# A four-layer graph attention network: moving the residual's end to GpSimd and shifting the preparation of some steps

## The chip, the cores and the metric

The kernel runs on one core of a Trainium2 chip. The metric is the device time of one execution in microseconds (us), as the median of several runs; less is better. The core has a matrix engine (TensorE, PE in the profile), a vector engine (VectorE, DVE), an activation engine (ScalarE, ACT), a general engine (GpSimd, POOL), a queue engine that issues transfers (SyncE, SP), and DMA engines. Each executes its own list of instructions in order, and they wait for each other by semaphores.

## The reference

Sixteen graphs (batches) of N = 1024 nodes with F = 256 features share one adjacency matrix. Four layers follow each other; each is

```
h   = max(layernorm(x), 0)
q   = h @ W                                    # heads: 4 of width 64 (layers 0, 2) or 1 of 256 (layers 1, 3)
e   = leaky_relu(e_src[i] + e_dst[j])          # e_src, e_dst = q times the two halves of a
att = softmax over j of e where adj[i, j], else -infinity
x   = x + elu(att @ q)                         # layers 0 to 2; relu instead of elu in layer 3
```

Layers 0 and 1 mask by adj > 0 and layers 2 and 3 by adj != 0. The slope of leaky_relu is 0.2, in layer 3 it is 0.01.

## The kernel before, in words

**Steps.** The work is cut into 64 steps, one for each pair of a graph and a layer. `order_of_steps` writes their order by hand: four streams, each of four graphs in turn, advance through the layers so that steps with four heads and steps with one head mostly alternate. The start is (graph, layer) = (0,0), (1,0), (2,0), (0,1), (3,0), (1,1), (2,1), (0,2), ..., and the end is step 57 (13,2), 58 (12,3), 59 (14,2), 60 (15,2), 61 (13,3), 62 (14,3), 63 (15,3). Only after steps 0, 1 and 59 does a step of four heads follow a step of four heads; the function `slack(n)` is true where one with one head follows.

**One step.** TensorE does the aggregation `att @ q` in eight groups (slots k = 0 to 7, L405). For each head and each of eight blocks of 128 source nodes, VectorE makes a tile w of 128 x 1024 weights (L389) from a broadcast row g, a column and the mask; 18 buffers ("w") hold such tiles. A step of four heads has 32 tiles, a step of one head 8, but both have about the same matrix work, so VectorE is the busier in the first kind and TensorE in the second, and the buffers carry the difference. ScalarE takes each group's sums from PSUM into y (L420). `finish(n)` then runs in the slots of the next step: a reciprocal of the softmax sums (L441, VectorE), the product y times r on GpSimd (L452; where `slack` and four heads, VectorE also makes min(y, 0) r at L451), the clamp min(y, 0) on GpSimd (L454), the exponential on ScalarE (L458), `max(e - 1, y)` on VectorE (L464) and the sum x + e on GpSimd (L465). The last layer has one VectorE instruction in place of the latter, `x = max(y, 0) + x` (L467), and then the store (L470) from SyncE, after which the next graph is loaded. Each of these comes twice, once for each half of the 1024 nodes.

**Preparation of a step** runs ahead, in 21 pieces: layernorm statistics of each half (L241, VectorE; four instructions a half), their combination on GpSimd (L268 to L280), normalising with relu (L286, ScalarE, four a half), a split into 16-bit halves (L295, ScalarE), a transposition by DMA (L297, issued by SyncE), a merge (L303, ScalarE), eight projections (L328, TensorE) with evictions on ScalarE (L330), exponentials for column and factor (L336, L338), a scaling on GpSimd (L340), the factors of the rows (L346, L347), a transposition of them (L352, L354) and a trip through DRAM (L356), from which they are fetched as rows gs (L372) and copied by ScalarE into PSUM as g (L384). In the steps n = 0 and 1 TensorE transposes instead (L317). Four PSUM banks ("bank") are shared by the group sums, the projections and the small transpositions, two more pairs hold g. Six buffers ("rows") are shared by normalised, split, turned and merged data and by e.

**What sets the order.** The program emits all instructions itself, in the order of emission for each engine. A table of 21 numbers says at which slot, counted from slot 8 (n - 2), each piece of step n's preparation is emitted: 0 and 1 are the statistics, 2 the combination, 3 and 4 normalising, 5 and 6 split and merge of half 0, 7 to 10 its projections, 11 to 16 the same for half 1, 17 to 20 the factors, rows and fetches. Steps with one head use ONE or TIGHT, with four heads SOON, FOUR, SHORT, NEXT; LATE is used where a step's input is finished too late (`free`). In each slot the order is: the w tiles that this group needs, the group, pieces of `finish`, broadcasts g, a weight piece from `later`, the preparation due, and more w tiles ahead. The start-up (masks, the first step's preparation) has a list of its own, `order`. `later` holds the pieces of `weight_columns` for layers 1 to 3: `vectors` fetches the attention vectors by a small DMA on SyncE (L143), `spread` broadcasts them by TensorE (L150, L153), `columns` and `bound` follow on VectorE, TensorE and GpSimd (L160, L161, L173 to L180).

Of the kernel before, what the change touches and what calls it, by code (L numbers as in the profile page):

```python
# [32 lines left out]
ALU = mybir.AluOpType  # L33
# [16 lines left out]
FOUR = (-8, -8, -5, 0, 1, 0, 3, 5, 5, 5, 5, 1, 4, 5, 5, 5, 5, 6, 8, 8, 10)  # L50
SHORT = (-4, -4, -4, 0, 1, 0, 3, 5, 5, 5, 5, 1, 4, 5, 5, 5, 5, 6, 8, 8, 10)
NEXT = (-4, -4, -4, 1, 3, 2, 5, 8, 8, 8, 8, 4, 7, 8, 8, 8, 8, 9, 10, 10, 12)
ONE = (2, 2, 2, 3, 4, 3, 5, 7, 7, 7, 7, 4, 7, 8, 8, 8, 8, 8, 11, 11, 12)
SOON = (0, 0, 0, 1, 2, 1, 3, 4, 4, 5, 5, 2, 5, 6, 6, 7, 7, 7, 8, 8, 10)
FIRST = (-4, -4, -4, -2, -0.9, -1, -1, -0.8, -0.8, -0.8, -0.8, 0, 0, 1, 1, 1, 1, 1, 2, 2, 4)
TIGHT = (4, 4, 4, 5, 6, 5, 7, 8, 8, 8, 8, 6, 8, 9, 9, 9, 9, 9, 10, 10, 12)
LATE = (0, 0, 0, 1, 2, 1, 3, 4, 4, 4, 4, 2, 4, 5, 5, 5, 5, 5, 6, 6, 8)


# [9 lines left out]
def kernel(ctx: ExitStack, tc: tile.TileContext, x, adj, ws, avs, out):  # L69
    nc = tc.nc  # L70
# [351 lines left out]
    def slack(n):  # L422

        return LAYERS[steps[n + 1][1]][0] == 1

    def finish(n):

        b, l = steps[n]
        H = LAYERS[l][0]
        D = F // H  # L430
        st = state[n]

        def views(half):
            s = slice(half * HALF, (half + 1) * HALF)
            return (xs[b][:, s, :].rearrange("p c (h d) -> p (c h) d", h=H),
                    st["y"][:, s, :, 0:D].rearrange("p c h d -> p (c h) d"),
                    st["r"][:, s, :].rearrange("p c h -> p (c h)"))

        def divide():
            st["r"] = small.tile([P, C, H], F32, name="r")  # L440
            nc.vector.reciprocal(st["r"], st["y"][:, :, :, D])  # L441

        def scaled(half):
            xh, yh, r = views(half)
            rb = r[:, :, None].to_broadcast([P, HALF * H, D])
            if l < L - 1:

                e = st["e", half] = prep.tile([P, HALF * H, D], F32, name="rows",
                                                    bufs=HBUFS)
                if H > 1 and slack(n):  # L450
                    nc.vector.scalar_tensor_tensor(e, yh, 0.0, rb, op0=ALU.min, op1=ALU.mult)  # L451
            nc.gpsimd.tensor_tensor(yh, yh, rb, op=ALU.mult)  # L452
            if l < L - 1 and not (H > 1 and slack(n)):
                nc.gpsimd.tensor_scalar(e, yh, 0.0, -3.0e38, op0=ALU.min, op1=ALU.max)  # L454

        def exponential(half):
            if l < L - 1:
                nc.scalar.activation(st["e", half], st["e", half], AF.Exp)  # L458

        def add(half):  # L460
            xh, yh, r = views(half)
            if l < L - 1:
                e = st["e", half]
                nc.vector.scalar_tensor_tensor(e, e, -1.0, yh, op0=ALU.add, op1=ALU.max)  # L464
                nc.gpsimd.tensor_add(xh, xh, e)  # L465
                return
            nc.vector.scalar_tensor_tensor(xh, yh, 0.0, xh, op0=ALU.max, op1=ALU.add)  # L467

        def store(half):
            nc.sync.dma_start(  # L470
                out=out[b].rearrange("(p c) f -> p c f", p=P)[:, half * HALF:(half + 1) * HALF],
                in_=xs[b][:, half * HALF:(half + 1) * HALF, :])
            if half == 1 and b + STREAMS < B:
                load(b + STREAMS)


        at = (0, 0, 0, 0, 1, 1, 1) if slack(n) and H > 1 else (0, 0, 1, 1, 2, 2, 3)
        return list(zip(at, (divide, lambda: scaled(0), lambda: scaled(1), lambda: exponential(0),
                             lambda: exponential(1), lambda: add(0), lambda: add(1)))) + (
                    [(4, lambda: store(0)), (4, lambda: store(1))] if l == L - 1 else [])  # L480

# [37 lines left out]
    def emit_heads(i):  # L519

        while done["g"] <= min(i + C // 2, done["tiles"] + C, len(tiles) - 1):
            n, h, _ = tiles[done["g"]]
            if n >= done["prepared"]:
                break
            broadcast(n, h)
            done["g"] += C
            fetch_heads()
# [13 lines left out]
    for n, (b, l) in enumerate(steps):  # L541

        free = -99
        if b % STREAMS in last:
            over = last[b % STREAMS] + 1
            free = 8 * over + (8 if l == 0 else 2 if LAYERS[steps[over][1]][0] == 1 else 4)
        last[b % STREAMS] = n
        start = 8 * (n - 2)
        kind = ONE if LAYERS[l][0] == 1 else SOON if n < 3 else FOUR
        if kind is FOUR and free > start + kind[0]:  # L550
            kind = SHORT if slack(n - 2) else NEXT
        if kind is ONE and free > start + kind[0]:
            kind = TIGHT
        if free > start + kind[0]:
            kind = LATE
            start = max(free, agenda_of[-1][0] + 5, start - LATE[7])
        agenda_of.append([start + k for k in kind] if n > 1 else FIRST)
        if n > 2:


            assert agenda_of[n][7] >= 8 * (n - 2)
            assert agenda_of[n][3] >= agenda_of[n - 1][12]
    ending = []
    later = {}
    with tc.manual_schedule():
        blocks = [mask_rows(c) for c in range(C)]
        layer = [weight_columns(l) for l in range(L)]
        layer[0][0](nc.scalar)
        load(0, 2)
        load_weights(0)  # L570
        for c in range(C):
            blocks[c][0]()
        load(1)
        load_weights(1)
        for i in range(2, STREAMS):
            load(i)
        nc.scalar.activation(warm, half1, AF.Exp)
        nc.vector.tensor_copy(identb, ident)
        layer[0][1]()
        first = [piece for _, piece in preparation(0)]  # L580

        order = (

            [first[0], first[1], first[3], lambda: layer[0][2](range(1)), first[2],
             lambda: layer[0][2](range(1, K)), first[5], first[6], first[4], layer[0][3]]

            + [blocks[c][1] for c in range(4)]
            + [first[7], first[8], blocks[0][2], blocks[4][1], blocks[5][1], blocks[0][3],
               first[9], first[10], blocks[1][2], blocks[6][1], blocks[7][1], blocks[1][3],
               first[11], first[12], blocks[2][2], blocks[0][4],  # L590
               lambda: prepare(-4), first[13], first[14], blocks[1][4], blocks[2][3],
               blocks[3][2], first[15], first[16], blocks[3][3]]

            + [first[17], blocks[4][2], first[18], first[19], lambda: emit_heads(0),
               blocks[5][2], blocks[6][2], blocks[4][3], blocks[4][4], blocks[5][3], blocks[5][4],
               blocks[6][3], blocks[7][2], blocks[2][4], blocks[3][4], blocks[7][3],
               lambda: prepare(-2), blocks[6][4], lambda: prepare(-1), blocks[7][4]])
        plan(1)
        planned = 2
        done["prepared"] = 1  # L600
        for piece in order:
            piece()
        emit_tiles(C, must=True)
        prepare(-0.5)
        for i in range(2, STREAMS):
            load_weights(i)

        for l, at in ((1, 1), (2, 8 * 3 + 3), (3, 8 * 5 + 3)):
            for i, piece in zip((0, 1, 2, 8), layer[l]):
                later[at + i] = piece  # L610
        for n in range(len(steps)):
            for k, (h, i0, per) in enumerate(groups(n)):
                while planned < len(steps) and min(
                        a[0] for a in agenda_of[planned:planned + 2]) <= 8 * n + k:
                    plan(planned)
                    planned += 1
                emit_tiles(place[n, h, C - 1] + 1, must=True)
                aggregate(n, h, i0, per)
                if i0 + per == C:
                    done["free"] = place[n, h, C - 1] + 1  # L620
                while ending and ending[0][0] <= k:
                    ending.pop(0)[1]()
                upto = min(done["tiles"] + (6 if per > 1 else 3), done["free"] + WBUFS)

                emit_heads(upto - 1 + (C // 2 if per == 1 and k >= C - 2 else 0))
                if 8 * n + k in later:
                    later[8 * n + k]()
                prepare(8 * n + k)
                emit_tiles(upto)
            for _, piece in ending:  # L630
                piece()
            ending = finish(n) if n < len(steps) - 1 else []
# [35 lines left out]
```

## Time and profile before

| what | value |
|---|---|
| median of 3 runs | 2464.47 us (2461.95 to 2467.52) |
| the profiled execution, its own time | 2463.54 us |
| its span, first to last instruction | 2461.8 us |
| mean granted TensorE clock | 0.994 |
| TensorE busy in 0 to 320 / 320 to 2240 / 2240 to 2462 us | 286.73 of 320 / 1904.05 of 1920 / 205.66 of 222 us |
| VectorE busy in the same stretches | 263.39 / 1630.99 / 146.77 us |
| one w tile (L389), mean of 1280 | 1273 ns |
| y times r on GpSimd (L452), mean of 126 | 2091 ns |
| scaling on GpSimd (L340), mean of 128 | 1913 ns |

The page gives for each engine the time that it was busy and its share of the span, the chain of work that ended last, and groups of instructions: line, engine, operation, output from inputs with their shapes, count, then busy us, mean ns of one, and the idle time ahead of them with what ended most of it. A view of the waits lists for an engine how long, how often and at most how long one line waited for what other engine and line. A timeline gives for each run of like instructions the start, the duration, and in brackets the idle time before and what ended it.

### The profile page before, as it was taken

The numbers are of one execution on the slowest core, as the hardware profiler recorded it, in microseconds if no ns is written. First come the engines' busy times: TensorE is split into PE (matmuls) and PEld (weight loads), VectorE is DVE, ScalarE is ACT, GpSimd is POOL, SyncE is SP. The second block draws the span as 40 slices with busy tenths as digits, with TensorE's granted clock in tenths as the row PEclk, the third lists the DMA queues.
The fourth block names the chain that finished last, engine by engine and source line by source line (L and its number), as shares of the span: only waits on it lengthen the run. The fifth ranks groups of instructions, "written<-read, shape, count | busy, mean of one in ns | idle before, by whom it ended". The sixth has DMA issues, their size and how long they took to land.

```text
span 2461.8 us, 86525 instructions
## 1 busy us (share of the span) xinstructions
PE 2396.4 (97%) x39104; PEld 2150.2 (87%) x39104; DVE 2041.2 (83%) x2138; ACT 1484.9 (60%) x2501; POOL 1074.7 (44%) x1366
## 2 busy tenths in 40 slices
PE   7989999999999999999999999999999999999899
PEld 5888798889898889898898888899988889888878
DVE  8988688888888988888988888988888888888963
ACT  5464676555666656765556765656665556765461
POOL 3344455543345454444343555453444344553341
PEclk9999999999999999999999999999999999999999
DMA  4322232233333322232433332323433422323221
GB/s 181 81 54 62 44 79 62 70 105 90 94 85 87 74 64 56 67 79 88 113 97 81 77 71 62 79 63 80 113 79 87 109 58 54 79 62 70 77 48 61
DMA packets 294761, 193.40 MB, mean 79 GB/s; under 512 B 264182, under 2 KB 266998, under 8 KB 292472
## 3 DMA queue, kind: packets, MB, share of 16 engines
q1 hardware_dynamic: 294382, 187.86, 30.2%
q8 instruction: 306, 5.01, 0.8%
q14 instruction: 63, 0.52, 0.1%
q10 hardware_dynamic: 10, 0.00, 0.0%
HBM read 105.39 MB, written 17.43 MB: 50 GB/s over the span
## 4 chain that ended last, share of the span: by engine, by line
PE 82%; ACT 6%; DVE 5%; DMA 4%; issue 2%; POOL 0%; SPq 0%; DVEq 0%; ACTq 0%
PE bank L405 64%; PE bank L328 18%; DVE w L389 4%; ACT rows L286 2%; DMA gs<-grow 2%; DMA grow<-gT 1%; ACT rows L295 1%; ACT g L384 1%; ACT rows L458 1%; ACT rows L303 1%; DVE bn L241 1%; ACT y L420 0%; DMA rows<-rows 0%; PE bank L352 0%; DVE rows L464 0%
## 5 line engine op out<-in xcount | busy, mean ns | idle before, releaser
L405 PE MATMUL bank<-whx,w 128*64 128x65 f32 x36864 | 1899.5, 240 | 26.4 <-DVE w L389 17.0
L405 PEld LDWEIGHTS bank<-whx,w 128*64 128x64 f32 x36864 | 1746.2, 144 | 186.5 <-issue 22.6
L389 DVE SCALAR_TENSOR_TENSOR w<-g,rcol,mask 128x1024 f32<-128x1024 f32 x1280 | 1538.9, 1273 | 206.1 <-PE bank L405 160.8
L340 POOL TENSOR_TENSOR whx<-whx 128x1024 f32<-128x1024 f32 x128 | 244.9, 1913 | 823.8 <-ACT whx L338 823.8
L420 ACT ACTIVATE y<-bank 128x260 f32<-128x260 f32 (+1 forms) x504 | 191.9, 381 | 567.1 <-PE bank L405 567.0
L328 PE MATMUL bank<-wx,rows 128*128 128x264 f32 (+1 forms) x2048 | 489.3, 393 | 16.0 <-ACT y L420 8.4
L328 PEld LDWEIGHTS bank<-wx,rows 128*128 128x128 f32 x2048 | 384.4, 192 | 92.5 <-ACT y L420 14.2
L452 POOL TENSOR_TENSOR y<-y,r 128x1024 f32<-128x1024 f32 x126 | 262.4, 2091 | 254.0 <-DVE rows L451 186.6
L330 ACT ACTIVATE whx<-bank 128x264 f32<-128x264 f32 (+1 forms) x512 | 193.6, 388 | 194.2 <-PE bank L328 193.5
L286 ACT ACTIVATE rows<-x,shift,rstd 128x256 f32<-128x256 f32 x512 | 264.5, 588 | 72.5 <-POOL shift L280 70.3
L465 POOL TENSOR_TENSOR x<-x,rows 128x1024 f32<-128x1024 f32 x96 | 227.1, 2365 | 181.6 <-DVE rows L464 181.6
L303 ACT ACTIVATE rows<-rows 128x2048 uint16<-128x2048 uint16 x124 | 265.9, 2144 | 21.5 <-DMA rows<-rows 21.5
L295 ACT ACTIVATE rows<-rows 128x2048 uint16<-128x2048 uint16 x124 | 236.9, 1911 | 3.9
L464 DVE SCALAR_TENSOR_TENSOR rows<-rows,y 128x1024 f32<-128x1024 f32 x96 | 187.9, 1957 | 49.1 <-ACT rows L458 43.7
L241 DVE BATCH_NORM_STATS2 bn<-x 128x6 f32<-128x256 f32 x512 | 175.5, 409 | 33.4 <-POOL x L465 30.0
L384 ACT ACTIVATE g<-gs 128x1024 f32<-128x1024 f32 x159 | 162.6, 1023 | 63.8 <-DMA gs<-grow 49.1
L274 POOL TENSOR_TENSOR rstd<-rstd,neghalf 128x4 f32<-128x4 f32 (+1 forms) x97 | 120.3, 1240 | 15.2 <-DVE shift L275 7.8
L458 ACT ACTIVATE rows<-rows 128x1024 f32<-128x1024 f32 x96 | 100.6, 1048 | 2.0 <-POOL rows L454 2.0
L441 DVE RECIPROCAL r<-y 128x32 f32<-128x32 f32 (+1 forms) x63 | 17.2, 274 | 96.3 <-ACT y L420 96.3
L451 DVE SCALAR_TENSOR_TENSOR rows<-y,r 128x1024 f32<-128x1024 f32 x58 | 70.1, 1250 | 1.1
L467 DVE SCALAR_TENSOR_TENSOR x<-y,x 128x1024 f32<-128x1024 f32 x30 | 36.5, 1215 | 8.9 <-POOL y L452 8.9
L338 ACT ACTIVATE whx<-whx,nbias 128x16 f32<-128x16 f32 (+1 forms) x128 | 40.3, 315 | 4.2
(67 smaller groups left out, 444.4 us busy)
## 6 DMA issues: line engine op xcount, KB each, us to landing
gs<-grow SPq DMA_DIRECT2D x159, 512.0 KB
x<-in_x SPq DMA_DIRECT2D x15, 1024.0 KB
out<-x SPq DMA_DIRECT2D x30, 512.0 KB
w<-in_adj SPq DMA_DIRECT2D x8, 512.0 KB
rows<-rows SPq DMA_TRANSPOSE x124
x<-in_x SPq DMA_DIRECT2D x2, 512.0 KB
wx<-in_L_gnn_W SPq DMA_DIRECT2D x8, 128.0 KB
out<-x SPq DMA_DIRECT2D x8, 128.0 KB
```

The costliest lines, as they stand in the source:

```text
L241: nc.vector.bn_stats(bn[:, c, :], xs[b][:, c, :])
L286: nc.scalar.activation(xn[:, :, q, :], xs[b][:, c, :].rearrange("p (k i) -> p k i", k=K), AF.Relu, bias=st["shift"][:, c:c + 1], scale=st[ ...
L295: nc.scalar.activation(bits, xn.rearrange("p (n s) -> p s n", s=2), AF.Copy)
L303: nc.scalar.activation(st["hT", half].rearrange("p k i -> p (k i)").bitcast(U16).rearrange("p (n s) -> p n s", s=2), st["turned", half].re ...
L328: nc.tensor.matmul(pw, lhsT=st["hT", half][:, k, q * P:(q + 1) * P], rhs=wx[l][:, k, :], start=(k == 0), stop=(k == K - 1))
L330: nc.scalar.activation(st["whx"][:, c, :], pw, AF.Copy)
L340: nc.gpsimd.tensor_tensor(wh[:, :, :, 0:D], wh[:, :, :, 0:D], wh[:, :, :, D:D + 1].to_broadcast([P, HALF, H, D]), op=ALU.mult)
L389: nc.vector.scalar_tensor_tensor(w, state[n]["g", h], state[n]["rcol"][:, jc, h:h + 1], masks[LAYERS[steps[n][1]][3]][:, jc, :], op0=ALU.m ...
L405: nc.tensor.matmul(acc[o % P:o % P + cols, q, :], lhsT=st["w", h, jc][:, o:o + cols], rhs=st["whx"][:, jc, h * (D + 1):(h + 1) * (D + 1)], ...
L420: nc.scalar.activation(st["y"][:, i0:i0 + per, h, :], acc, AF.Copy)
L452: nc.gpsimd.tensor_tensor(yh, yh, rb, op=ALU.mult)
L465: nc.gpsimd.tensor_add(xh, xh, e)
```

## The change: what it does

1. In the last layer, `add` is no longer a VectorE instruction: GpSimd clamps y at 0 right after its product (in `scaled`), and adds it to x in `add`.
2. In a step of four heads that is followed by one of four heads (n = 0, 1 and 59), `add` has four GpSimd instructions for a half in place of one of VectorE and one of GpSimd: y = max(y, 0), x = x + y, e = e - 1, x = x + e.
3. The table SOON is used for n < 8 and not only for n < 3, so for steps 4 and 7 instead of FOUR and SHORT: their statistics come at slots 16 and 40, where they came at 8 and 36; normalising and the split and merge of step 4 move by one slot or stay. SOON itself has new numbers, which step 2 feels: its two merges both at slot 4, its projections all at slot 5, the factors at 6 and not 7.
4. TIGHT has every number one higher, which steps 3 and 62 use: all of their preparation comes one slot later (the statistics of step 3 at slot 13 and not 12).
5. The 4 in `free` becomes 5. With that step 60 is planned by LATE from slot 461 instead of NEXT from slot 464: its statistics come at slot 461 (before 460), normalising at 462 and 463 (465 and 467), merges at 464 and 465 (469 and 471), projections at 465 and 466 (472), rows at 467 (474).
6. The attention vectors of layers 2 and 3 are fetched one slot sooner, at slots 26 and 42 and not 27 and 43; spread, columns and bound stay where they were.
7. In the start-up, the eight mask transpositions of block 5 stand ahead of the transposition of the first step's row factors.

```diff
-SOON = (0, 0, 0, 1, 2, 1, 3, 4, 4, 5, 5, 2, 5, 6, 6, 7, 7, 7, 8, 8, 10)
+SOON = (0, 0, 0, 1, 2, 1, 4, 5, 5, 5, 5, 2, 4, 5, 5, 5, 5, 6, 8, 8, 10)
...
-TIGHT = (4, 4, 4, 5, 6, 5, 7, 8, 8, 8, 8, 6, 8, 9, 9, 9, 9, 9, 10, 10, 12)
+TIGHT = (5, 5, 5, 6, 7, 6, 8, 9, 9, 9, 9, 7, 9, 10, 10, 10, 10, 10, 11, 11, 13)
...
             nc.gpsimd.tensor_tensor(yh, yh, rb, op=ALU.mult)
+            if l == L - 1:
+                nc.gpsimd.tensor_scalar(yh, yh, 0.0, 3.0e38, op0=ALU.max, op1=ALU.min)
...
             if l < L - 1:
                 e = st["e", half]
+                if H > 1 and not slack(n):
+
+                    nc.gpsimd.tensor_scalar(yh, yh, 0.0, 3.0e38, op0=ALU.max, op1=ALU.min)
+                    nc.gpsimd.tensor_add(xh, xh, yh)
+                    nc.gpsimd.tensor_scalar(e, e, -1.0, -3.0e38, op0=ALU.add, op1=ALU.max)
+                    nc.gpsimd.tensor_add(xh, xh, e)
+                    return
                 nc.vector.scalar_tensor_tensor(e, e, -1.0, yh, op0=ALU.add, op1=ALU.max)
                 nc.gpsimd.tensor_add(xh, xh, e)
                 return
-            nc.vector.scalar_tensor_tensor(xh, yh, 0.0, xh, op0=ALU.max, op1=ALU.add)
+            nc.gpsimd.tensor_add(xh, xh, yh)
...
-            free = 8 * over + (8 if l == 0 else 2 if LAYERS[steps[over][1]][0] == 1 else 4)
+            free = 8 * over + (8 if l == 0 else 2 if LAYERS[steps[over][1]][0] == 1 else 5)
...
-        kind = ONE if LAYERS[l][0] == 1 else SOON if n < 3 else FOUR
+        kind = ONE if LAYERS[l][0] == 1 else SOON if n < 8 else FOUR
         if kind is FOUR and free > start + kind[0]:
             kind = SHORT if slack(n - 2) else NEXT
+        if kind is SOON and free > start:
+            kind = SHORT
...
-            + [first[17], blocks[4][2], first[18], first[19], lambda: emit_heads(0),
-               blocks[5][2], blocks[6][2], blocks[4][3], blocks[4][4], blocks[5][3], blocks[5][4],
+            + [first[17], blocks[4][2], blocks[5][2], first[18], first[19], lambda: emit_heads(0),
+               blocks[6][2], blocks[4][3], blocks[4][4], blocks[5][3], blocks[5][4],
...
-        for l, at in ((1, 1), (2, 8 * 3 + 3), (3, 8 * 5 + 3)):
-            for i, piece in zip((0, 1, 2, 8), layer[l]):
+        for l, at in ((1, 1), (2, 8 * 3 + 2), (3, 8 * 5 + 2)):
+            for i, piece in zip((0, 1, 2, 8) if l == 1 else (0, 2, 3, 9), layer[l]):
```

## The prediction

> **What bounds the kernel now.** I read the page's busy times and the chain that ended last first, then the costliest groups:
>
> ```profile
> PE 2396.4 (97%) x39104; PEld 2150.2 (87%) x39104; DVE 2041.2 (83%) x2138; ACT 1484.9 (60%) x2501; POOL 1074.7 (44%) x1366
> ...
> PE 82%; ACT 6%; DVE 5%; DMA 4%; issue 2%; POOL 0%; SPq 0%; DVEq 0%; ACTq 0%
> ...
> L465 POOL TENSOR_TENSOR x<-x,rows 128x1024 f32<-128x1024 f32 x96 | 227.1, 2365 | 181.6 <-DVE rows L464 181.6
> ...
> L464 DVE SCALAR_TENSOR_TENSOR rows<-rows,y 128x1024 f32<-128x1024 f32 x96 | 187.9, 1957 | 49.1 <-ACT rows L458 43.7
> ...
> L467 DVE SCALAR_TENSOR_TENSOR x<-y,x 128x1024 f32<-128x1024 f32 x30 | 36.5, 1215 | 8.9 <-POOL y L452 8.9
> ```
>
> TensorE is busy for 97% of the span: only its idle 65 us (2461.8 less 2396.4) and half-clock time can change. So next TensorE's waits by stretch: 0 to 320 us, 320 to 2240, and 2240 to the end.
>
> ```profile
> PE bank L405 <- DVE w L389: 10.8, 13, 0.9
> PE bank L317 <- ACT rows L286: 7.2, 2, 3.7
> PE bank L150 <- DMA w<-in_L_gnn_a: 7.0, 3, 4.6
> ```
>
> ```profile
> PE bank L328 <- ACT y L420: 7.7, 10, 2.5
> PE bank L405 <- issue: 4.8, 8, 1.2
> ```
>
> ```profile
> PE bank L405 <- DVE w L389: 6.2, 9, 0.9
> ...
> PE bank L328 <- ACT rows L303: 2.6, 1, 2.6
> ```
>
> VectorE's tiles are waited for only in the first and last stretch. In the middle VectorE itself waits, and for TensorE:
>
> ```profile
> DVE w L389 <- PE bank L405: 145.3, 26, 6.7
> ```
>
> **What the Trainium skill says.** "GPSIMD Engine Reference", section 3.1, puts a GpSimd tensor_tensor at 1.96 times VectorE's. The trace agrees: 2.365 us (L465) against 1.215 (L467). "SBUF — State Buffer", "Who interferes with whom": a VectorE instruction with two SBUF inputs and a GpSimd instruction that reads SBUF exclude each other. L464 takes about 1.2 us alone and 2.91 at 271.51 beside L452; the mean of 1957 ns lies between. "TensorE: Matmul & The Clock Gate", "HAM oscillation": a wait across a clock window halves the clock for the next. The trace has such windows, even after short waits:
>
> ```profile
> 203.87 1.24 PE L150 MATMUL bank<-w,ones 1*128 1x512 f32 x2 [1.30 <-DMA w<-in_L_gnn_a]
> 205.04 12.18 PE L405 MATMUL bank<-whx,w 128*128 128x257 f32 x48
> ```
>
> Such 48 matmuls take 10.59 us elsewhere, so that window cost 1.6 to 1.7 us.
>
> **Part by part.** Which instruction stands behind which on an engine is read from the two programs as built. The sum starts from the profiled execution, 2463.54 us (span 2461.8 and 1.7 around it), 0.93 below the median of 2464.47.
>
> Residual of the last layer. Thirty L467 go: 30 x 1.215 = 36.5 us of VectorE. GpSimd gets 30 adds at 2.365 and 30 one-input clamps at about 1.04 (L454's duration): 102 us on an engine with 1387 us idle. In the middle that is worth 0, because VectorE waits 145.3 us for buffers there; the store, which stands last, has nothing on TensorE behind it in that step. Bounds -1 to +1. It matters only in the DVE-bound stretch 2281 to 2303, where two L467 stand ahead of late tiles: -2.4.
>
> elu's end in three steps (n = 0, 1, 59). Six L464 go. For each half GpSimd does two clamps and two adds, 2 x 1.04 + 2 x 2.365 = 6.8 us instead of 2.4. For steps 0 and 59 VectorE is behind:
>
> ```profile
> 100.36 2.65 DVE L241 BATCH_NORM_STATS2 bn<-x 128x6 f32<-128x256 f32 x8
> ...
> 112.51 1.22 DVE L464 SCALAR_TENSOR_TENSOR rows<-rows,y 128x1024 f32<-128x1024 f32 x1
> ```
>
> Removed ahead of the 80th tile: two L464 at 1.15 and, since its statistics move behind that tile, the fifth step's L241 (2.65): -4.95. The fourth step's statistics need GpSimd's sums: from about 108 us on, 2 x 6.8 = 13.6 gives 122, and VectorE reaches them at 122 to 123: just covered; up to +1.5 if it is not. For step 59, two L464 before 2344: -2.3.
>
> Start-up order. Eight mask transposes move ahead of the gcol transpose, whose wait of 1.26 us at 31.65 they fill: -1.2.
>
> Third step (n = 2). Both merges (L303) now stand together in slot 4, ahead of two L384 and the fifth group's L420 on ScalarE, which is in order. The second merge waits for its DMA transposition. A split takes about 5.5 us to reach its merge; the second split ends at 70.26, SyncE is held until 76.4, so it lands between 75 and 79. Then 2.14 (merge) + 1.02 (g) + 0.4 must pass before a PSUM bank comes free. TensorE has four banks, one with the group's sums, so it does three projections (3 x 0.98) and stops near 77.1 until 80 to 82.5: 2.9 to 5.4 us, against 0.97 + 1.16 that go. At the 80th tile, with the start-up's gain and the -4.95, VectorE is 1.9 to 3.6 ahead (2.8).
>
> Second step (n = 1). The fourth step's preparation is a slot later, so on ScalarE the first exponential now stands ahead of its first four evictions (L330). It waits for L441, L452 and L454 on GpSimd (0.3 + 1.9 + 1.04). TensorE with four full banks waits from about 144.0 to 148.2: +4.2 us, and a half-clock window with even chance, +0.9. Its queue behind: L336, L338, the merge, the L420s. Net of the start: -2.8 + 4.2 + 0.9 = +2.3 (from -5.8, the wait hidden and no half clock, to +4.0).
>
> Vectors of layers 2 and 3, one slot sooner. Each is one small DMA, moved ahead of queued fetches and transpositions on SyncE, which it delays by its issue alone (0: their users wait for more than that). The 1.30 goes and its half-clock window: -3.0. The 1.17 at 287.10 goes too, counted next.
>
> Eighth step (n = 7). Its L241 moves from 253.03 to behind the L441 and L451 of step 4, near 270. GpSimd's combining (4.2 us) then stands behind both L452 and an L340: ends near 279 instead of 260. ScalarE's L286 starts at 279 instead of 273.4, its second merge ends near 294.9 instead of 290.85. The projection, which began at 291.70, waits 2.6 to 3.6; less the 1.17 partly: +2.5 (0 to +3.6). VectorE's waits at 249 to 253 stay: the moved L241 lies behind them.
>
> Step 60 now is planned early. Its combining on GpSimd stands behind both L340 of step 59, which end at 2236.2, so it ends at about 2238.2 to 2240 instead of 2232.5. L286 and L295 follow to about 2242 to 2244, transposition to 2247.7, merge to 2250. TensorE is ready for it at 2245.6 (one group into step 58): +4.4, and +0.9 for half a clock window. Before, this projection ran without a wait:
>
> ```profile
> 2270.37 7.39 PE L328 MATMUL bank<-wx,rows 128*128 128x264 f32 x32
> ```
>
> VectorE can't use that stall, since its 18 buffers are full again before 2277. Two reliefs follow, -2.4 and -2.3 as above. Step 62 a slot later hides the 2.62 us at 2361.25 and its 1.7 of half clock: -4.3. In its place step 62's g (L384) falls behind the merge of step 63 and comes 3 to 5 us later, where 1.2 us were to spare: +2.8. This end: 5.3 - 4.7 - 4.3 + 2.8 = -0.9; since the reliefs overlap with "issue" gaps in the same stretch I take +1.0, from -9 (no stall) to +7.
>
> Sum: 2.3 - 3.0 + 2.5 + 1.0 + 0 = +2.8, so 2466.3 for a profile like this one and 2467.3 on the median's scale. About 0.2% (2459.5 to 2469.4) is what a measurement can tell from no change. My forecast is no change that can be told, its own range 2462 to 2472.
>
> **Rivals.** Slower, by ScalarE's order: every new wait (merge behind a transposition, exponential ahead of evictions, late L286, step 60's merge) costs its upper end and a half-clock window. It decides as soon as ScalarE is held longer than three projections take, 2.9 us, since the four banks are then full. Start +4.0, vectors -1.2, eighth step +3.6, end +7: +13.4, 2478. For it: "L328 <- ACT y" is the middle's largest wait already. Against it: ScalarE is 40% idle, and single waits are short.
>
> Faster, by relief: transpositions land early and ScalarE catches up, so VectorE's tiles come sooner wherever TensorE waited for them. Start -5.8, vectors -3.0 with 1.17 at 287: -4.2, end -2 to -6: -12 to -16; with half of the start kept back, -11: 2453.5. For it: the 17 us that TensorE waits for tiles lie just where work is taken off. Against it: the new order puts waits in their place.
>
> That the large item does nothing, the 36.5 us taken off VectorE, is in all three: 28 of 30 stand where VectorE waits for buffers.
>
> **How the numbers follow.** No change 0.38; slower 0.38 (the rival and the upper part of the forecast's own range); faster 0.24. The range runs from half of the faster case (2455) to the slower one (2478), leaving out one in ten at each end.
>
> **What would show it.** Right: TensorE's "L405 <- DVE w" falls from 17.0 to under 10; "L150 <- DMA w" falls by 2.5; new waits on ScalarE of 3 to 5 us near 77, 144, 292 and 2246; the middle's pair of steps stays at 74.1 us; L465 and its neighbours grow by about 100 us on GpSimd. Wrong: no L328 wait over 2 us at those places (then faster), or L389 waits that stay (then slower), or a store or fetch on SyncE that GpSimd's adds hold back, which would show as "L384 <- DMA gs" in the middle.

## The result, and the profile after

The changed kernel takes 2496.55 us (median of 4 runs, 2496.11 to 2497.11), against 2464.58 for the kernel before beside it (2461.95 to 2467.52): ratio 1.0127, 95% interval 1.0114 to 1.0139. It is 32 us slower. "No change", 2467.3, was forecast, and the range ended at 2478.

Where the 32 us arise can be seen from one mark in both traces: the end of the eviction of each step's last group (L420). Their differences, after less before, worked out from one trace of each (us):

| end of step | difference | since the line above |
|---|---|---|
| 0 | +4.7 | +4.7 |
| 1 | +4.8 | +0.1 |
| 2 | +16.1 | +11.3 |
| 4 | +16.6 | +0.5 |
| 5 | +21.8 | +5.2 |
| 6 to 48 | +22.1 to +24.4 | about +2.5 over 43 steps |
| 49 to 56 | +21.1 to +21.7 | about -3 |
| 57 | +25.6 | +4.3 |
| 62 | +33.1 | +7.5 |

So nearly everything happens in the first six and the last seven steps. (Step 58 itself stands at +36.3, because step 60's projections now run in it and no longer in step 59.) The middle is all but untouched, as forecast, although 24 of the 30 VectorE instructions that went over to GpSimd stand between 320 and 2240 us.

The same parts of the page as before, the busy times and the chain, and its rows for the residual (L454 is the new clamp on GpSimd, L476 the addition, L473 and L474 what is left of the old L464 and L465):

```profile
PE 2406.1 (96%) x39104; PEld 2153.6 (86%) x39104; DVE 1999.3 (80%) x2102; ACT 1487.8 (60%) x2501; POOL 1306.1 (52%) x1444
...
PE 73%; ACT 7%; DMA 4%; POOL 3%; DVE 2%; issue 2%; SPq 0%; ACTq 0%; POOLq 0%; DVEq 0%
...
L474 POOL TENSOR_TENSOR x<-x,rows 128x1024 f32<-128x1024 f32 x90 | 213.7, 2375 | 161.7 <-DVE rows L473 161.7
...
L473 DVE SCALAR_TENSOR_TENSOR rows<-rows,y 128x1024 f32<-128x1024 f32 x90 | 177.9, 1977 | 34.4 <-ACT rows L460 29.9
...
L454 POOL TENSOR_SCALAR y<-y 128x1024 f32<-128x1024 f32 x30 | 109.0, 3634 | 2.6
...
L476 POOL TENSOR_TENSOR x<-x,y 128x1024 f32<-128x1024 f32 x30 | 65.4, 2198 | 0.0
```

VectorE lost 42 us of work and TensorE gained nothing: GpSimd's share of the chain rose from 0 to 3%. And a clamp takes 3634 ns, where 1.04 us was assumed. The groups of GpSimd by line show that it is not a matter of size; L456 is the old clamp min(y, 0), L468 and L470 are the new max(y, 0) and e - 1 at elu's end:

```profile
L456 POOL TENSOR_SCALAR rows<-y 128x1024 f32<-128x1024 f32 x38 | 39.6, 1042 | 3.3
L470 POOL TENSOR_SCALAR rows<-rows 128x1024 f32<-128x1024 f32 x6 | 21.9, 3645 | 0.5
L468 POOL TENSOR_SCALAR y<-y 128x1024 f32<-128x1024 f32 x6 | 21.8, 3640 | 0.3
```

TensorE's waits of the changed kernel, in 0 to 320 us:

```profile
PE bank L405 <- DVE w L389: 15.5, 12, 8.3
PE bank L328 <- ACT y L420: 6.7, 3, 5.1
PE bank L328 <- ACT rows L303: 6.6, 2, 4.8
```

from 320 to 2240, much as before:

```profile
PE bank L405 <- issue: 6.4, 9, 1.4
PE bank L328 <- ACT y L420: 5.5, 8, 1.6
```

and after 2240:

```profile
PE bank L405 <- DVE w L389: 10.1, 9, 5.2
PE bank L328 <- ACT rows L303: 4.4, 2, 4.1
```

The waits for tiles were to fall below 10 us in all; they rose from 17.0 to 25.7, and single ones are 8.3 and 5.2 us long. VectorE's timeline shows why. It has come to the fourth step's statistics:

```profile
124.31 1.40 DVE L241 BATCH_NORM_STATS2 bn<-x 128x6 f32<-128x256 f32 x4
134.85 1.41 DVE L241 BATCH_NORM_STATS2 bn<-x 128x6 f32<-128x256 f32 x4 [9.15 <-POOL x L471]
```

Its tiles for step 1 stand behind the second line, and TensorE waits for them until 137.50. In the table step 1 loses only 0.1 us all the same: without this wait it makes up the stall of step 0 (with the fast forms of a later run its end is 4.8 us earlier than before, and not 4.8 later). GpSimd meanwhile, the second half of step 0's end:

```profile
122.77 3.63 POOL L468 TENSOR_SCALAR y<-y 128x1024 f32<-128x1024 f32 x1
126.49 2.19 POOL L469 TENSOR_TENSOR x<-x,y 128x1024 f32<-128x1024 f32 x1
128.76 3.64 POOL L470 TENSOR_SCALAR rows<-rows 128x1024 f32<-128x1024 f32 x1
132.48 2.34 POOL L471 TENSOR_TENSOR x<-x,rows 128x1024 f32<-128x1024 f32 x1
```

A half takes 3.63 + 2.19 + 3.64 + 2.34 = 11.8 us and gaps, a step's end 24.3 us (110.53 to 134.82). In step 2 the same four instructions for step 1's data stand between GpSimd's other work until 191.39. There ScalarE's normalising of step 4 waits for it:

```profile
177.44 2.09 ACT L286 ACTIVATE rows<-x,shift,rstd 128x256 f32<-128x256 f32 x4 [7.83 <-POOL x L471]
```

L286 works on another graph than L471; what ties them are the six "rows" buffers, which hold normalised data and e alike (L471, which reads the e of step 1's first half, ends at 177.41). TensorE then waits for the merge (L303):

```profile
184.25 9.07 PE L328 MATMUL bank<-wx,rows 128*128 128x264 f32 x32 [4.84 <-ACT rows L303]
```

The same 32 matmuls took 7.39 us at 169.88 in the kernel before; the granted clock was 0.50 from 186 to 188, so a half-clock window follows the wait here too.

Step 5's +5.2 has another place. TensorE waits there for a PSUM bank whose eviction stands on ScalarE behind step 7's normalising, and the next 16 matmuls take 5.42 us, which took 3.74 before:

```profile
306.21 1.09 PE L150 MATMUL bank<-w,ones 1*128 1x512 f32 x2 [3.68 <-ACT y L420]
```

### The profile page after: what moved, and what is told of

It reads as the page before. It is cut to its first block, busy times and chain, and to the rows that moved or that the text cites. A ratio compares the mean times of both kernels' runs of the same rounds, so it can differ in the third digit from the quotient of the medians.

```text
span 2494.9 us, 86583 instructions
## 1 busy us (share of the span) xinstructions
PE 2406.1 (96%) x39104; PEld 2153.6 (86%) x39104; DVE 1999.3 (80%) x2102; ACT 1487.8 (60%) x2501; POOL 1306.1 (52%) x1444
## 4 chain that ended last, share of the span: by engine, by line
PE 73%; ACT 7%; DMA 4%; POOL 3%; DVE 2%; issue 2%; SPq 0%; ACTq 0%; POOLq 0%; DVEq 0%
PE bank L405 57%; PE bank L328 16%; ACT rows L286 2%; DMA gs<-grow 2%; DMA grow<-gT 2%; DVE w L389 1%; ACT rows L295 1%; ACT g L384 1%; DMA rows<-rows 1%; ACT rows L460 1%; ACT rows L303 1%; ACT y L420 1%; DVE rows L473 0%; POOL whx L340 0%; POOL x L474 0%
## 5 line engine op out<-in xcount | busy, mean ns | idle before, releaser
L405 PE MATMUL bank<-whx,w 128*64 128x65 f32 x36864 | 1907.4, 241 | 39.0 <-DVE w L389 25.7
L420 ACT ACTIVATE y<-bank 128x260 f32<-128x260 f32 (+1 forms) x504 | 192.2, 382 | 571.0 <-PE bank L405 570.7
L328 PEld LDWEIGHTS bank<-wx,rows 128*128 128x128 f32 x2048 | 385.7, 193 | 106.0 <-ACT rows L303 21.1
L286 ACT ACTIVATE rows<-x,shift,rstd 128x256 f32<-128x256 f32 x512 | 265.4, 591 | 101.6 <-POOL shift L280 92.1
L474 POOL TENSOR_TENSOR x<-x,rows 128x1024 f32<-128x1024 f32 x90 | 213.7, 2375 | 161.7 <-DVE rows L473 161.7
L303 ACT ACTIVATE rows<-rows 128x2048 uint16<-128x2048 uint16 x124 | 265.9, 2145 | 29.8 <-DMA rows<-rows 29.7
L473 DVE SCALAR_TENSOR_TENSOR rows<-rows,y 128x1024 f32<-128x1024 f32 x90 | 177.9, 1977 | 34.4 <-ACT rows L460 29.9
L384 ACT ACTIVATE g<-gs 128x1024 f32<-128x1024 f32 x159 | 162.8, 1024 | 57.0 <-DMA gs<-grow 52.8
L454 POOL TENSOR_SCALAR y<-y 128x1024 f32<-128x1024 f32 x30 | 109.0, 3634 | 2.6
L476 POOL TENSOR_TENSOR x<-x,y 128x1024 f32<-128x1024 f32 x30 | 65.4, 2198 | 0.0
```

The lines of the kernel that those rows point to most:

```text
L286: nc.scalar.activation(xn[:, :, q, :], xs[b][:, c, :].rearrange("p (k i) -> p k i", k=K), AF.Relu, bias=st["shift"][:, c:c + 1], scale=st[ ...
L303: nc.scalar.activation(st["hT", half].rearrange("p k i -> p (k i)").bitcast(U16).rearrange("p (n s) -> p n s", s=2), st["turned", half].re ...
L328: nc.tensor.matmul(pw, lhsT=st["hT", half][:, k, q * P:(q + 1) * P], rhs=wx[l][:, k, :], start=(k == 0), stop=(k == K - 1))
L384: nc.scalar.activation(g, state[n]["gs", h], AF.Copy)
L405: nc.tensor.matmul(acc[o % P:o % P + cols, q, :], lhsT=st["w", h, jc][:, o:o + cols], rhs=st["whx"][:, jc, h * (D + 1):(h + 1) * (D + 1)], ...
L420: nc.scalar.activation(st["y"][:, i0:i0 + per, h, :], acc, AF.Copy)
```

## The experiments

Theory 1: GpSimd's price for the new forms makes x of steps 0, 1 and 59 late, and that is the larger part of the loss. Theory 2: ScalarE's order by the new tables is the larger part. Each kernel ran beside the kernel before, whose median was 2460 to 2465 us; ratios are compared, not times of different sets.

**GpSimd's forms alone** (a kernel of its own).

> The network is left out: fifteen graphs are copied to the output, and on the first one GpSimd alone runs sixteen elementwise forms over 128 x 1024 floats, three times each. In the changed kernel the clamps max(y, 0) and e - 1 took 3.64 us each, the clamp min(y, 0) takes 1.04. Three guesses: (in place) writing over its own input costs it, then every form in place takes 3.64 and every form into another tile 1.04; (order) only a min followed by a max is fast, then min(y, 3e38) followed by max(0) in place takes 1.04 and the max, min pair 3.64 wherever it writes; (stride) the pitch of 65 or 257 in the output costs it, which the e - 1 on a contiguous tile speaks against.

Measured, GpSimd's timeline, the second of the three times for the first forms, in the order in which they ran (L39 is min(0) then max(-3e38) into another tile; L40 max(0) then min(3e38) into another tile; L46 is as L39 from a pitch of 257; L41 min(3e38) then max(0); L47 add(-1) then max(-3e38) in place; L42 as L40 in place; L43 as L41 in place; L49 add(-1) then a product with 1; L51 a single addition):

```profile
125.13 1.04 POOL L39 TENSOR_SCALAR e<-y 128x1024 f32<-128x1024 f32 x1
126.13 3.63 POOL L40 TENSOR_SCALAR d<-y 128x1024 f32<-128x1024 f32 x1
129.72 1.04 POOL L46 TENSOR_SCALAR e<-y 128x1024 f32<-128x1024 f32 x1
130.72 1.04 POOL L41 TENSOR_SCALAR d<-y 128x1024 f32<-128x1024 f32 x1
131.85 3.64 POOL L47 TENSOR_SCALAR e<-e 128x1024 f32<-128x1024 f32 x1
135.56 3.63 POOL L42 TENSOR_SCALAR y<-y 128x1024 f32<-128x1024 f32 x1
...
142.99 1.04 POOL L43 TENSOR_SCALAR y<-y 128x1024 f32<-128x1024 f32 x1
144.10 1.04 POOL L49 TENSOR_SCALAR d<-e 128x1024 f32<-128x1024 f32 x1
...
152.08 2.78 POOL L51 TENSOR_SCALAR d<-e 128x1024 f32<-128x1024 f32 x1
```

The pair of operations decides, and its order: min then max 1.04 us, max then min 3.63, in place or not, from a pitch of 65 and of 257. Addition then max takes 3.64, addition then product 1.04, and a single addition or max 2.78. The guesses "in place" and "stride" are refuted; why the forms differ is not shown. So the same values were to be had at 1.04 us.

**Elu's end given back to VectorE.**

```diff
-                if H > 1 and not slack(n):
-                    nc.gpsimd.tensor_scalar(yh, yh, 0.0, 3.0e38, op0=ALU.max, op1=ALU.min)
...
-                    return
                 nc.vector.scalar_tensor_tensor(e, e, -1.0, yh, op0=ALU.add, op1=ALU.max)
```

> The changed kernel with elu's end of steps 0, 1 and 59 given back to VectorE, everything else as changed. Theory 1 (the price of GpSimd's clamps: 2 x (3.64 + 2.19 + 3.64 + 2.37) = 23.7 us for a step's end where 13.6 were assumed, so x of steps 0, 1 and 59 is late): some 12 to 18 us of the 32 come back, 2479 to 2485, the start's offset behind step 2 falls from 16 to 5 or less, and the 9.15 us wait of VectorE for GpSimd's sums at 125.7 is gone. Theory 2 (ScalarE's order by the new tables): under 5 us come back, above 2491.

Measured: 2476.26 us, 1.0058 (1.0046 to 1.0070). By the ratios 17 us (1.0127 less 1.0058) of the 32 come back, as theory 1 had it (in microseconds the run lies below its range); step 2's offset is 3.1 instead of 16.1, and TensorE's longest wait for a tile is 0.9 us.

**Elu's end alone, in the kernel before** (the same lines added to it).

> The kernel before with elu's end of steps 0, 1 and 59 moved to GpSimd, nothing else changed. Theory 1: VectorE waits for GpSimd's sums ahead of the statistics of the fourth step, and ScalarE and TensorE after it: 2472 to 2482. Theory 2: within 4 us of before, 2461 to 2469.

Measured: 2483.82 us, 1.0094 (1.0075 to 1.0114), somewhat more than theory 1 had. VectorE's timeline has the same wait without any new table:

```profile
131.45 1.41 DVE L241 BATCH_NORM_STATS2 bn<-x 128x6 f32<-128x256 f32 x4 [8.84 <-POOL x L469]
```

**The residual alone, in the kernel before** (L454 and L476 of the change).

```diff
+            if l == L - 1:
+                nc.gpsimd.tensor_scalar(yh, yh, 0.0, 3.0e38, op0=ALU.max, op1=ALU.min)
...
-            nc.vector.scalar_tensor_tensor(xh, yh, 0.0, xh, op0=ALU.max, op1=ALU.add)
+            nc.gpsimd.tensor_add(xh, xh, yh)
```

> The kernel before with only the last layer's residual moved to GpSimd. Both theories: the middle doesn't feel it although each clamp takes 3.64 us, since VectorE waits for buffers there and GpSimd is half idle; 2461 to 2466. If GpSimd's later sums hold the stores and the fetches behind them on SyncE, it is above 2470, and ScalarE's g waits for gs.

Measured: 2459.43 us, 0.9985 (0.9977 to 0.9994): a small gain, just below the range of both theories, with clamps of 3.63 us. The middle doesn't feel it. After 2240 us TensorE waits less for tiles than before (6.2 us there):

```profile
PE bank L405 <- DVE w L389: 3.5, 5, 0.9
```

**The changed kernel with the fast forms.**

```diff
-nc.gpsimd.tensor_scalar(yh, yh, 0.0, 3.0e38, op0=ALU.max, op1=ALU.min)
+nc.gpsimd.tensor_scalar(yh, yh, 3.0e38, 0.0, op0=ALU.min, op1=ALU.max)
...
-nc.gpsimd.tensor_scalar(e, e, -1.0, -3.0e38, op0=ALU.add, op1=ALU.max)
+nc.gpsimd.tensor_scalar(e, e, -1.0, 1.0, op0=ALU.add, op1=ALU.mult)
```

> The changed kernel with the same values by other forms: max(y, 0) as min(y, 3e38) and then max with 0, and e - 1 as an addition of -1 and then a product with 1. Both took 1.04 us where they were measured alone, against 3.63. A step's end on GpSimd is then 2 x (1.04 + 2.19 + 1.04 + 2.36) = 13.3 us, what the prediction had assumed. Theory 1 (the price of the forms): nearly all of what giving elu back to VectorE brought, 2464 to 2474. Rival (four instructions in a row, and the x of these steps late by GpSimd's queue whatever one costs): above 2482.

Measured: 2479.96 us, 1.0056 (1.0043 to 1.0070), beside a before of 2465.37: in microseconds between theory 1's range and the rival's, but by the ratio it brings as much as giving elu back (1.0058). The statistics at 123.76 have no wait ahead of them:

```profile
123.76 2.69 DVE L241 BATCH_NORM_STATS2 bn<-x 128x6 f32<-128x256 f32 x8
```

**Elu's end alone in the kernel before, fast forms.**

> The kernel before with only elu's end of steps 0, 1 and 59 on GpSimd, in the forms of 1.04 us. The same move with the forms of the change gave a ratio of 1.0094 (1.0075 to 1.0114). Theory (price alone): 0.998 to 1.001. Rival (four instructions in GpSimd's queue hold the fourth step's statistics whatever they cost): 1.004 or more.

Measured: 2460.19 us, 0.9998 (0.9990 to 1.0006), where the slow forms gave 1.0094. The move, its place in the queue and the order are the same; only the forms differ. So its loss is the price, and the queue costs nothing that can be told.

**The third step's table given back** (from here on elu's end is on VectorE again; n = 2 uses the old numbers of SOON).

```diff
+THIRD = (0, 0, 0, 1, 2, 1, 3, 4, 4, 5, 5, 2, 5, 6, 6, 7, 7, 7, 8, 8, 10)
...
-        kind = ONE if LAYERS[l][0] == 1 else SOON if n < 8 else FOUR
+        kind = ONE if LAYERS[l][0] == 1 else THIRD if n == 2 else SOON if n < 8 else FOUR
```

> The kernel with elu's end back on VectorE (2476.3 us), and in addition the third step's preparation at its old slots. Theory: ScalarE's second merge, behind its DMA transposition and ahead of g and an eviction, costs 4.9 us at 76.7 and half a clock window; without it step 0 ends 4 to 5 us sooner, of which 3 to 6 us reach the end: 2470 to 2473. Rival (VectorE's tiles set the pace by step 2 anyway): 2475 to 2477.

Measured: 2475.74 us, 1.0041 (1.0028 to 1.0053), so 0.17% less than 1.0058, though the intervals overlap; in microseconds it lies where the rival had it, so by itself this run doesn't decide. At the end of step 0 its offset is -1.6 us instead of +4.1, but at the end of step 5 only 3 us of these 5.7 are left. In the changed kernel TensorE had done three projections (x12) and stopped:

```profile
74.21 2.94 PE L328 MATMUL bank<-wx,rows 128*128 128x264 f32 x12
82.21 6.41 PE L328 MATMUL bank<-wx,rows 128*128 128x264 f32 x20 [5.07 <-ACT y L420]
```

**The eighth step's table given back, by one edit.**

```diff
-        kind = ONE if LAYERS[l][0] == 1 else SOON if n < 8 else FOUR
+        kind = ONE if LAYERS[l][0] == 1 else SOON if n < 7 else FOUR
```

> The kernel with elu's end back on VectorE (2476.3 us), and in addition the eighth step's statistics at slot 36 again. Theory: late statistics make GpSimd's combination, ScalarE's normalising and both merges late in step 5; the step's offset to the kernel before grows there from 3.1 to 8.3, and that goes: 2470 to 2472. Rival (the offset comes from the vectors fetched sooner, or from the stall of earlier steps): 2475 to 2477.

Measured: 2489.78 us, 1.0099 (1.0085 to 1.0113): 10 us slower than with elu's end given back alone, a miss. The edit did something else. With `free` one slot later, step 7 no longer fits SHORT and falls to LATE, with its projections at slots 43 and 44 where they stood at 45 before (not 41 and 42, as the next run but one expects). TensorE stops for the merge:

```profile
290.48 6.71 PE L328 MATMUL bank<-wx,rows 128*128 128x264 f32 x16 [5.96 <-ACT rows L303]
```

It shows what a preparation planned too early costs, but tells nothing of the change's table for this step.

**Step 60's table given back.**

```diff
-            free = 8 * over + (8 if l == 0 else 2 if LAYERS[steps[over][1]][0] == 1 else 5)
+            free = 8 * over + (8 if l == 0 else 2 if LAYERS[steps[over][1]][0] == 1 else 4)
```

> The kernel with elu's end back on VectorE (2476.3 us), and in addition step 60's preparation at its old slots. Theory: the wait of 4.1 us for its first merge in step 58 and the half clock after it go, and g of step 59 isn't late; of the end's growth of 6.6 us (4.4 to 11.0) 3 to 6 go: 2470 to 2473. Rival (VectorE's tiles set the end's pace, so the stall is hidden): 2475 to 2477.

Measured: 2472.34 us, 1.0033 (1.0020 to 1.0045), 0.25% less than 1.0058. In the changed kernel the wait and, after it, a half-clock window were there; 16 matmuls took 6.43 us here and 3.75 us at 2281.58:

```profile
2271.84 6.43 PE L328 MATMUL bank<-wx,rows 128*128 128x264 f32 x16 [4.11 <-ACT rows L303]
```

**Steps 7 and 60 given back** (the last two edits together, so that step 7 uses SHORT).

> The kernel with elu's end back on VectorE, and steps 7 and 60 both prepared at their old slots (the run that was to give step 7 back alone had planned it a second way, projections at slot 41 and 42, since its input counts as ready one slot later: it stopped TensorE for 5.96 us at 284.5). What is left of the tables is the third, fourth, fifth and 62nd step. Theory: both steps' stalls go, ratio to before 1.000 to 1.003 (step 60 alone gave 1.0033). Rival (step 7's late statistics are hidden): 1.0033 or more.

Measured: 2468.54 us, 1.0025 (1.0016 to 1.0035). Against 1.0033 that leaves some 2 us for step 7 by itself, within the intervals. The traces show the place: the wait at step 5's L150 is 1.15 us here and 3.05 with step 60 alone given back, and what step 5 loses falls from 4.1 to 1.6 us.

**Steps 2, 7 and 60 given back** (the third step's edit and the last two together; the later slots of n = 3, 4 and 62 are left).

> Elu's end on VectorE, steps 2, 7 and 60 prepared at their old slots; of the tables only the third, fourth and 62nd step's later slots are left. Steps 7 and 60 alone gave 1.0025. Theory (the third step's stall of some 5 us is the rest): 0.9985 to 1.000, no slower than before. Rival (the later slots of steps 3 and 4 put an exponential on GpSimd's sums ahead of TensorE's evictions, 4.1 us near 146): 1.001 to 1.0025.

Measured: 2463.57 us, 1.0011 (1.0002 to 1.0020). Against 1.0025 the third step is worth 0.14%, but a rest remains, as the rival had it. Its trace has the rival's wait, ScalarE's evictions (here L331) behind an exponential:

```profile
148.17 6.55 PE L406 MATMUL bank<-whx,w 128*64 128x65 f32 x128 [4.14 <-ACT whx L331]
```

128 such matmuls take 3.95 us elsewhere: half clock again (0.50 from 148 to 152). The other part of the rest is step 62. Its first tile comes at 2389.19, where it came at 2384.52 in the kernel without new tables (three runs below), because its g now stands on ScalarE behind the merge of step 63; all eight kernels with the later slot lose 3.3 us or more in step 62, and the six without it nothing. The wait of 2.62 us at 2361.25, which the later slot was to hide, is 2.45 here; only the half clock after it is gone.

**Only the start-up's order and the vectors** (the last two hunks of the change's diff, in the kernel before).

> The kernel before with only the vectors fetched one slot sooner and the start-up's order. The prediction: -1.2 for the start-up and -3.0 for the vectors (the waits of 1.30 and 1.17 us at 203.87 and 287.10 and a half-clock window go): 0.998 to 0.9992 of before. Rival (another wait ends last in both places): 1.000.

Measured: 2461.13 us, 1.0001 (0.9992 to 1.0010): nothing, as the rival had it. In its trace the wait at the first L150 is gone and step 3 ends 5.4 us earlier, but step 5 only 2.4: the second one still waits, and now a half-clock window follows there (16 matmuls in 5.42 us, 3.74 before):

```profile
282.96 1.09 PE L150 MATMUL bank<-w,ones 1*128 1x512 f32 x2 [1.18 <-DMA w<-in_L_gnn_a]
283.99 5.42 PE L405 MATMUL bank<-whx,w 128*128 128x257 f32 x16
```

**Residual with the fast clamp, start-up and vectors, all tables as before** (the run above, and in it the residual's two hunks with min(3e38) then max(0)).

> The kernel before with only the parts that add no wait: the last layer's residual on GpSimd, with the clamp in its 1.04 us form, the vectors fetched one slot sooner, and the eight mask transpositions moved ahead in the start-up; all tables as before, elu's end on VectorE. Theory (the tables' order on ScalarE costs what is left): faster than before by 3 to 7 us, ratio 0.997 to 0.9988. Rival (the tables are harmless and one of these three costs): slower than before.

Measured: 2457.83 us, 0.9990 (0.9981 to 1.0000): not slower, so the rival is out, but the gain is just short of the range, and no more than the residual brings alone (0.9985).

**The same, with elu's end on GpSimd in the fast forms** (the lines of the run on elu's end alone).

> As the kernel without the tables (residual, vectors, start-up), and in addition elu's end of steps 0, 1 and 59 on GpSimd with the 1.04 us forms. Theory (by the price alone, 13.3 us of GpSimd for a step's end instead of 2 x 2.36 after VectorE's): VectorE gains 2 x 1.15 ahead of the late tiles and loses what the statistics of the fourth step wait, since they stand at slot 12: within 4 us of the kernel without it. If the price of 23.7 us was the only fault of elu's end, it is as fast or faster; if the queue on GpSimd costs as well, it is slower by over 4 us.

Measured: 2457.28 us, 0.9985 (0.9975 to 0.9995). This version beats both kernels, by 3 us against before, but so does the residual alone, by as much; whether elu's end, the vectors or the start-up add anything can't be told.

## Why the prediction was wrong, step by step

The 32 us are, by the ratios of the runs, some 17 for GpSimd's price, some 17 for the tables, and a few microseconds gained elsewhere.

**The price.** The term that failed first is "two clamps and two adds, 2 x 1.04 + 2 x 2.365 = 6.8 us" for a half of elu's end. Adds took 2.19 and 2.36, but clamps 3.64, so a half takes 11.8 us. The 1.04 was the row of L454 in the kernel before, a min followed by a max; the change has a max followed by a min and an addition followed by a max, which no row of the trace before showed. It was taken as the same operation. No second bound was set, though the price was 3.5 times as high. From this term all else of that part follows: the sums end at 134.8 and not at 122, the cover "just covered; up to +1.5" is exceeded by VectorE's 9.15 us, and TensorE's 8.3. Before step 61 it comes again (VectorE waits 7.39 us, TensorE 5.24). That the price is the cause is shown by taking elu's end out (1.0127 to 1.0058, 17 us) and, in the kernel before, by changing the forms alone (1.0094 to 0.9998).

"Second step: +4.2" was right in place and size where the price isn't in the way (4.14 us with the slots of steps 3, 4 and 62 alone). What was not foreseen is the wait of ScalarE's L286 for a "rows" buffer held by step 1's end; it comes from the same price (7.83 us, 2.66 with the fast forms, none with elu's end on VectorE).

**The tables, and what was set against them.** "Third step: 2.9 to 5.4 us" was right, 5.07. "Step 60: +4.4 and half a clock window" was right, 4.11, and the window came. For the eighth step the place was another: the projection waited only 0.68, and the 3.68 us stood two instructions earlier, at L150. The tables cost some 0.7%, or 17 us (1.0058 against 0.9990 without them). The prediction's own terms for them sum to 9.5 to 12: 2.9 to 5.4 less 2.13 for the third step, less 2.65 for the fifth step's statistics, 5.1 for the second, 2.5 for the eighth, 5.3 for step 60, and -4.3 + 2.8 for step 62. Of the 17, step 60 carries about 0.25% (6 us), the third step 0.14 to 0.17%, the eighth perhaps 0.1% (forecast +2.5 us), steps 3, 4 and 62 what remains (1.0011 against 0.9990: 0.2%, 5 us). In this remainder the "+2.8" came, as 3.3, and the "-4.3" came only in its half-clock part.

Against the tables the forecast set 11.2 us of other reliefs (2.3 and 2.3 from elu's end, 1.2 from the start-up, 3.0 from the vectors, 2.4 from the residual). With the fast forms and without the tables, all of these together brought 3.7 us (0.9985), which the residual brings alone. So the second step that failed is the netting: the forecast took the middle of each wait and the whole of each relief. The rival "slower, by ScalarE's order" named this mechanism and its places, and with +13.4 nearly the tables' size. (The "2.8" by which VectorE was to be ahead at the 80th tile can't be had from the terms shown; they give 2.9 to 5.4. That is 1.3 us, and changes nothing here.)

"Residual: 0 in the middle, -2.4 at the end" was right: 0.9985, so -3.7 with an interval from -1.5 to -5.7. Its clamps were under-priced in the same way (clamps and additions took 174 us of GpSimd and not 102), but GpSimd had the time.

"Start-up -1.2" was about right at its place: with start-up and vectors alone step 0 ends 2.3 us before that of before's trace, but 0.8 to 1.2 also in three runs that leave the start-up as it was. "Vectors -3.0" was half right: the wait of 1.30 at the first L150 went, the other one did not, and the half-clock window that was saved in one place came in the other. Together nothing was left at the end.

Open: why GpSimd's forms differ in price, and how steps 3 and 4 share what they cost.

## What to carry to other kernels

The price of an instruction belongs to its form, the pair of operations and their order included: a row for "a two-operation instruction on this engine and size" doesn't price another pair, and where the trace has no row, a bound on the high side is due. A gain on an engine that is not the bound is worth only what TensorE waited for it, while a late engine with a queue in order passes its delay on to all that share its buffers. New waits of TensorE mostly reached the end, often with a half-clock window more (step 60: 4.1 us of wait, 6 at the end); most reliefs did not: another wait then ended last, or a half-clock window came elsewhere (the vectors, step 62).

## What the runs showed of the hardware that was not expected

**GpSimd's forms.** On GpSimd a tensor_scalar over 128 x 1024 floats took 1.04 us as min then max, add then multiply, or multiply then add (1.05), 2.78 us as a single add or max, and 3.63 us as max then min or add then max. In the Trainium skill, "GPSIMD Engine Reference", section 7, gives 4 cycles an element for a dependent chain of floats, and section 3.1 a floor of 1.03 cycles for short loop bodies; at 1.2 GHz (section 1) 1024 elements would be 3.4 and 0.9 us, an estimate that lies near the slowest and the fastest forms, but not near the 2.78 us of a single operation. That this is the cause in these forms is not shown.

**TensorE's half clock.** In the 15 traces of the network, each stretch of granted clock 0.50 begins on a grid of 3.41 us, and all but those that the end cuts short last one or several such windows. TensorE's idle time was added up window by window, from 45 us on and up to 15 us before the end (the ends of matmuls are modelled by the profile): each of the 84 windows at full clock that were followed by half clock held at least 1.15 us of it; of the 10346 followed by full clock 132 held more than 1.15, and none more than 1.94. That accounts for the two short waits for the vectors. In the run with start-up and vectors alone the second one, 281.78 to 282.96, lies in one window (280.70 to 284.11), and half clock follows from 284.11 to 287.52. In the kernel before the same wait, 285.93 to 287.10, is cut by a window's edge at 286.60 into 0.67 and 0.50 us, and the clock stays full. The prediction had "a wait across a clock window" halve it; in these traces the wait must fill enough of one window. So moving a wait by a microsecond can bring or save a loss of 1.7 us (16 matmuls in 5.42 us and not 3.74). What decides between 1.15 and 1.94 us is not known.
